# A decoder layer on one core: the layernorms' reciprocal root by Newton's method instead of ScalarE's Sqrt table

## The chip, the core and the metric

The kernel runs on one core of one Trainium2 chip. The core has five engines that run their own queues of instructions in order: TensorE (PE, matrix products and transposes; PEld is its loading of weights), VectorE (DVE), ScalarE (ACT), GpSimd (POOL) and SyncE (SP, which here issues most transfers). Engines wait for each other by semaphores. Operands lie in the on-chip memory SBUF (128 partitions); products land in PSUM, which has eight banks of 128 x 512 numbers.

The metric is device time in microseconds (us) of one execution. A profiled execution gives the rows quoted below. ScalarE computes a function such as exp, gelu or square root out of a table; where the next function lies in another table, the profile shows an ACT_TABLE_LOAD.

## The reference

A transformer decoder layer with normalisation ahead of each part, in f32, on x of shape (4, 1024, 256) and a context of (4, 64, 256):

```python
x = x + self_attention(layernorm(x))             # 16 heads of 16, 1024 x 1024 scores per head
x = x + cross_attention(layernorm(x), context)   # 16 heads of 16, 64 context tokens
x = x + ffn(layernorm(x))

def layernorm(x):  return (x - mean(x)) / sqrt(var(x) + 1e-5)
def self_attention(x):
    q, k, v = split(x @ W_qkv + b_qkv)
    return (softmax(q @ k.T) / 16 @ v) @ W_out + b_out       # per head
def ffn(x):
    h = gelu(x @ ternary(W_fc).T)
    h = layernorm(h) * ln_w + ln_b                          # over 1024
    return h @ ternary(W_proj).T
```

`ternary` turns a weight matrix into -1, 0 and 1 by a threshold from its mean absolute value. So each of the 4 batches has three layernorms of x (the first, second and third) and one of the hidden h.

## The kernel before

Tokens lie on partitions, 128 at a time: a batch b is NT = 8 tiles of 128 x 256. The work has three stages.

*The beginning* (to about 50 us) normalises batch 0, projects q and k of the first heads, and stores them to DRAM (`kept_q`, `kept_k`), from where `fetch(u)` brings them back in the layout of the scores, on SP's queue.

*The attention* (to about 1098 us) is a loop over 16 units u = (batch b, group g of four heads) of 16 steps each. A step makes scores for one pair of heads (`scores`, two products that each are followed by a product with `sel` and `mT`, which subtracts the row's maximum), exp on ACT (L888), the scores of the second pair and their exps, then `weigh`, which multiplies exps by the values into `ps_acc`. Between them `top()` makes scores of the next unit once more the other way round, only for the maxima that DVE reduces (L433). Scores, maxima and all side work share a ring of seven PSUM banks; PE waits when ACT or DVE has not yet emptied the bank that comes next.

The side work is written as generators in three lines. `due` holds `ln1(b)` (the first layernorm and the transposes of the next batch), `project` and `values`; `later` holds `context` and `value_bias` (once) and `post(b)` (output projection, second layernorm, cross-attention, statistics and root of the third layernorm); `aside` makes the ternary weights. `fill(kind, n)` is called twice a step and steps at most n of these generators to their next `yield`. A yield tagged "rows" or "cols" needs PE and a place of that kind; one tagged "free" has no product behind it, and each line takes at most one of these in a call. So a "free" yield that nothing stands behind is an empty place: it lets half a step go by.

The order on PE and SP is that of the program (`ordered`). The order on ACT, DVE and POOL is chosen by the framework's scheduler, from its own estimate of when operands are ready; it may move an instruction ahead of others written earlier.

*The last stage* (from about 1098 us) has the FFN in eight halves of four tiles: `widen(i)` normalises x with the kept root `rs3`, multiplies by `wfc`, applies gelu on ACT (L1001, tile `h`), takes the statistics (L1004, L1005), the root (L1007), the scale's product `nmr` (L1009), and normalises h, two tiles on DVE (L1012) and two on ACT (L1015). `narrow(i)` transposes h, splits it on ACT (`hT`, L1035) and DVE (`hl`, L1036) into a rounded part and its rest, and multiplies by `wproj`. A fixed list of places (`WIDE`, `NARROW`) puts them in each other's gaps, together with the rest of batch 3's `post`. There a step that is tagged "Gelu" or "Sqrt" is held back while a group of four cross-attention exps is open, so that their tables do not alternate (`apart`).

A layernorm is three helpers. `ln_stats` takes mean and variance on DVE (L233, L234: tile `mv`). `ln_rstd` (L236 to L240) makes the root on ACT (`sd`, with a table load at L239 where the table is another) and the reciprocal on DVE. `ln_normalised` (L242 to L260) makes `xn`: in the attention (`state["split"]`) by ACT as scale * x + bias (L250), with the bias `nmr` made on DVE (L246); elsewhere on DVE (L256).

POOL does little: copies of the cross-attention's weights (L463, `xwk` and `xwq`), `bv_wide` (L529), `lnb_wide` (L764), and the additions of the output biases to x (`add_row`, L280, with `bo`, `xbo` and `yrow`).

Of the kernel before, what the change touches and what calls it, by code (L numbers as in the profile page):

```python
# [8 lines left out]

F32 = mybir.dt.float32  # L10
F32R = mybir.dt.float32r
DRAM = bass.MemoryType.DRAM
AF = mybir.ActivationFunctionType
ALU = mybir.AluOpType
# [7 lines left out]
P = 128  # L22
NT = S // P
NG = 4
NU = B * NG
LN_EPS = 1e-5
# [4 lines left out]
def decoder_layer(ctx, tc, a, out):  # L31
# [48 lines left out]
    def xs(t, n=1):  # L80

        return x_of[t // NT][:, t % NT : t % NT + n, :]
# [95 lines left out]

    state = {"split": False, "banks": "ring"}

    def bank():
        return ps[state["banks"]]()
# [49 lines left out]
            nc.vector.bn_aggr(out=mv[:, i, :], in_=st)  # L234

    def ln_rstd(pool, rs, mv):  # L236
        n = mv.shape[1]
        sd = pool.tile([P, n], F32, tag="sd", name="sd", bufs=2)
        nc.scalar.activation(sd, mv[:, :, 1], AF.Sqrt, bias=eps_t[:, 0:1])  # L239
        nc.vector.reciprocal(out=rs, in_=sd)  # L240

    def ln_normalised(pool, mv, rs, i, t, n):  # L242
        xn = pool.tile([P, n, E], F32, tag="xn", name="xn", bufs=2)
        if state["split"]:
            nmr = pool.tile([P, n], F32, tag="nmr", name="nmr", bufs=2)
            nc.vector.scalar_tensor_tensor(  # L246
                nmr, mv[:, i : i + n, 0], -1.0, rs[:, i : i + n], ALU.mult, ALU.mult
            )
            for k in range(n):
                nc.scalar.activation(  # L250
                    xn[:, k, :], xs(t + k)[:, 0, :], AF.Identity, bias=nmr[:, k : k + 1],
                    scale=rs[:, i + k : i + k + 1],
                )
            return xn
        for k in range(n):
            nc.vector.tensor_scalar(  # L256
                xn[:, k, :], xs(t + k)[:, 0, :], mv[:, i + k, 0:1], rs[:, i + k : i + k + 1],
                ALU.subtract, ALU.mult,
            )
        return xn  # L260
# [63 lines left out]
    def ln1(b):  # L324
        mv = main.tile([P, NT, 2], F32, tag="mv1", name="mv1", bufs=2)
        rs = main.tile([P, NT], F32, tag="rs1", name="rs1", bufs=2)
        xnT_of[b] = xnT = main.tile([P, 2, S], F32, tag="xnT", name="xnT")
        n = NT if state["split"] else NT // 2
        for i0 in range(0, NT, n):
            for i in range(i0, i0 + n, 2):  # L330
                yield "free"
                ln_stats(main, mv, [(i + k, b * NT + i + k) for k in range(2)])
            yield "free"
            ln_rstd(main, rs[:, i0 : i0 + n], mv[:, i0 : i0 + n, :])
            for i in range(i0, i0 + n, 4):
                yield "free"
                xn = ln_normalised(post_pool, mv, rs, i, b * NT + i, 4)
                yield "rows"
                ln_transposed(xnT[:, :, i * P : (i + 4) * P], xn)

# [199 lines left out]
    def post(b):  # L540
# [20 lines left out]
        for i in range(0, NT, 2):  # L561
            yield "free"
            ln_stats(post_pool, mv, [(i + n, t0 + i + n) for n in range(2)])
        yield "free Sqrt"
        ln_rstd(post_pool, rs, mv)
        for half in range(2):
            h0 = half * 4
            xnT = post_pool.tile([P, 2, 512], F32, tag="xn2T", name="xn2T")
            yield "free"
            xn = ln_normalised(post_pool, mv, rs, h0, t0 + h0, 4)  # L570
            add_row(t0 + h0, xbo, 4)
            yield "rows"
            ln_transposed(xnT, xn)
            q2 = post_pool.tile([P, 2, 512], F32, tag="q2", name="q2")
            m = 256 if state["split"] else 512
            for i in range(0, 512, m):
                for c in range(2):
                    yield "cols+" if c or i else "cols"
                    head_proj(q2[:, c, :], late["xwq"], late["xbq"], c, xnT, slice(i, i + m))
            nm = post_pool.tile([P, 4, 2, 8], F32, tag="nm2", name="nm2")  # L580
            for t in range(4):
                yield "rows"
                pm = two_banks()
                for c in range(2):
                    for s in range(2):
                        r = slice(64 * s, 64 * s + 64)
                        matmul(
                            pm[s][:, c * 256 : (c + 1) * 256], lhsT=q2[r, c, t * P : (t + 1) * P],
                            rhs=kx[r, c, b, :, :].rearrange("p j k -> p (j k)"), start=True, stop=True,
                        )  # L590
                for s in range(2):
                    nc.vector.tensor_reduce(  # L592
                        nm[:, t, s, :], pm[s].rearrange("p (h k) -> p h k", k=SK), AX.X, ALU.max,
                        negate=True,
                    )
            yield "free"
            dst = nm_x[:, :, :, 0:8, :]
            nc.vector.tensor_copy(dst[:, :, :, :, 0].bitcast(F32R), nm)
            nc.vector.tensor_tensor(dst[:, :, :, :, 1], nm, dst[:, :, :, :, 0], ALU.subtract)
            yield "rows"  # L600
            views = turned([nm_x[:, t, :, :, :].rearrange("p s h l -> p (s h l)") for t in range(4)])
            mT = post_pool.tile([P, 512], F32R, tag="mTx", name="mTx")
            for r, v in enumerate(views):
                nc.scalar.copy(mT.rearrange("p (k r i) -> p r k i", r=len(views), k=4)[:, r, :, :], v)
            att = post_pool.tile([P, 4, NG, NG * D], F32, tag="attx", name="attx")
            before = None
            for g in range(NG):
                yield "rows+" if g else "rows"
                pe = two_banks()
                c, q = divmod(g, 2)  # L610
                sides = [(p, slice(64 * p, 64 * p + 64)) for p in range(2)]
                for p, r in sides:
                    matmul(
                        pe[p], lhsT=kx[r, c, b, 2 * q : 2 * q + 2, :].rearrange("p n k -> p (n k)"),
                        rhs=q2[r, c, :], start=True, stop=False,
                    )
                for p, r in sides:
                    matmul(
                        pe[p], lhsT=sel_x[r, 2 * g : 2 * g + 2, :].rearrange("p n k -> p (n k)"),
                        rhs=mT[r, :], start=False, stop=True,  # L620
                    )
                yield "free Exp"
                ex = post_pool.tile([P, 2, 512], F32, tag="xn2T", name="ex")
                for p in range(2):
                    nc.scalar.activation(ex[:, p, :], pe[p], AF.Exp, scale=0.25)  # L625
                if before is not None:
                    yield "rows"
                    normalised(*before)
                yield "cols"
                pa = bank()  # L630
                for j in range(NG):
                    matmul(
                        pa[32 * j : 32 * j + 32, :], lhsT=vx[:, b, 2 * g + j // 2, j % 2, :],
                        rhs=ex[:, j // 2, :], start=True, stop=True,
                    )
                oT = post_pool.tile([P, 512], F32, tag="oT", name="oT", bufs=2)
                nc.scalar.copy(oT, pa)
                before = att[:, :, g, :].rearrange("p t (j e) -> p t j e", j=NG), oT
            yield "rows"
            normalised(*before)  # L640
            yield from projected(
                lambda c, t: att[:, t, 2 * c : 2 * c + 2, :].rearrange("p g d -> p (g d)"),
                late["xwo"], t0 + h0, 4,
            )
        sl = slice(t0, t0 + NT)
        for i in range(0, NT, 2):
            yield "free"
            ln_stats(post_pool, mv3[:, sl, :], [(i + n, t0 + i + n) for n in range(2)])
        yield "free Sqrt"
        ln_rstd(post_pool, rs3[:, sl], mv3[:, sl, :])  # L650
        if b < B - 1:
            dma(out=x_kept[:, sl, :], in_=x_of[b])
# [174 lines left out]
        next(parts)  # L827
    run(first)
    run(parts)
    state["split"] = True  # L830
    run(fetch(0))

    sel_f = post_pool.tile([P, 2, P], F32, tag="xn", name="sel_f", bufs=2)
# [142 lines left out]
    def widen(i):  # L976
# [14 lines left out]
        for t in range(NH):  # L991
# [11 lines left out]
            for half in range(2):  # L1003
                nc.vector.bn_stats(out=st[:, half, :], in_=h[:, t, half * 512 : (half + 1) * 512])  # L1004
            nc.vector.bn_aggr(out=mv[:, t, :], in_=st)  # L1005
        yield "Sqrt"
        ln_rstd(ffn, rs, mv)  # L1007
        nmr = ffn.tile([P, NH], F32, tag="nmr", name="nmr", bufs=2)
        nc.vector.scalar_tensor_tensor(nmr, mv[:, :, 0], -1.0, rs, ALU.mult, ALU.mult)  # L1009
# [73 lines left out]
    while tag is not None or narrows:  # L1083
# [6 lines left out]
        if wides:  # L1090
            i = halves - len(wides)
            first = len(wides[0].places) <= len(WIDE) - 2
            late_x = i >= 2 * (B - 1) and tag is not None
            full = first and len(narrows) > halves + 1 - i
            apart = exps % NG and tag is not None and wides[0].tag in ("Gelu", "Sqrt")
            if not (late_x or full or apart):
                sources.append(wides[0])
        if narrows and len(narrows) > len(wides):
# [65 lines left out]
```

## Time and profile before

| | us |
|---|---|
| median of three runs | 1366.59 |
| lowest and highest | 1365.82, 1367.46 |
| the profiled execution | 1365.17 |
| its span | 1363.4 |
| table loads on ACT (43) | 1.283 each |
| root on ACT (`sd`, 21) | 0.30 each |
| reciprocal on DVE (`rs`, 21) | 0.18 to 0.19 each |
| `nmr` on DVE in the attention (12) | 0.154 each |
| addition of a bias on POOL, 128x512 | 1.30 each |

A row of the profile's groups names the source line, engine, operation, the tiles written and read, their shapes and the count; behind the first bar stand the busy time in us and the mean of one in ns, behind the second the idle time of the engine ahead of these instructions and what ended it. A row of the timeline gives start and duration in us, engine, line, operation, tiles and count; in brackets the idle time ahead of it and what ended that ("issue": nothing that the profile shows). The slices cut the span in 40; a digit is tenths of busy time, for PEclk tenths of the full clock of TensorE. The chain follows the work that ended last back to its start.

### The profile page before, as it was taken

To read this page: it belongs to the slowest core of one execution; us is meant where nothing else is said; L and a number is where in the kernel's file an instruction comes from. 1 tells how busy PE (TensorE), PEld (TensorE's weight loads), DVE (VectorE), ACT (ScalarE), POOL (GpSimd) and SP (SyncE) were. 2 spreads that over 40 slices of the span, in tenths; PEclk is the share of its full clock that TensorE was granted. 3 is DMA by queue.
4 is the path that set the end of the run, shared out by engine and by line. 5 is a ranking of instruction groups with operands and counts; after the bars stand their busy time and mean duration, and the time that the engine had idled before them with its cause. 6 is when DMAs were issued, how large, how long until landed. Compare 5 with 4: busy or idle time off the path is not lost.

```text
span 1363.4 us, 27651 instructions
## 1 busy us (share of the span) xinstructions
PE 1282.1 (94%) x11000; PEld 717.4 (53%) x11000; DVE 1004.7 (74%) x2110; ACT 898.5 (66%) x1654; POOL 80.0 (6%) x86
## 2 busy tenths in 40 slices
PE   3879999999999999999999999999999988999987
PEld 1434445545545454444545544545455466776777
DVE  4877777867878877877877777878889357565665
ACT  1377666756687667777676676676766746474765
POOL 4000000003010000011000000010000012000000
PEclk9889999999999999989999999999999989999989
DMA  5440312312130202131212112212210010100000
GB/s 169 126 143 30 111 42 68 94 48 63 41 85 1 63 7 57 33 93 31 64 35 60 38 27 75 82 53 73 55 40 1 2 62 1 44 19 31 1 31 32
DMA packets 46064, 72.72 MB, mean 53 GB/s; under 512 B 11280, under 2 KB 27920, under 8 KB 45936
## 3 DMA queue, kind: packets, MB, share of 16 engines
q1 hardware_dynamic: 44720, 68.47, 17.0%
q8 instruction: 87, 1.43, 0.4%
q10 hardware_dynamic: 1072, 2.10, 0.4%
q0 software_dynamic: 144, 0.39, 0.2%
q14 instruction: 41, 0.34, 0.1%
HBM read 46.81 MB, written 24.12 MB: 52 GB/s over the span
## 4 chain that ended last, share of the span: by engine, by line
PE 73%; DVE 16%; ACT 8%; issue 2%; DMA 1%; SPq 0%; DVEq 0%; ACTq 0%
PE ps_ring L57 42%; PE ps_acc L57 15%; PE ps_wide L57 8%; DVE mx L433 8%; PE ps_misc L57 3%; ACT exp L888 3%; PE ps_misc L60 2%; PE ps_ring L60 2%; DVE nm L592 2%; ACT xn L250 1%; DVE xn L256 1%; DVE bn L233 1%; DMA x<-in_x 1%; ACT ex L625 1%; ACT hl L359 1%
## 5 line engine op out<-in xcount | busy, mean ns | idle before, releaser
L433 DVE TENSOR_REDUCE mx<-ps_ring 128x1 f32<-128x512 f32 x1024 | 646.4, 682 | 157.6 <-PE ps_ring L57 156.7
L888 ACT ACTIVATE exp<-ps_ring 128x512 f32<-128x512 f32 x1024 | 549.2, 606 | 191.1 <-PE ps_ring L57 187.5
L57 PE MATMUL ps_ring<-q,k 64*128 64x512 f32 x1024 | 280.5, 474 | 8.0 <-ACT exp L888 5.9
L57 PE MATMUL ps_ring<-k,q 64*128 64x512 f32 x1024 | 260.2, 425 | 20.1 <-DMA q<-kept_q 7.9
L57 PE MATMUL ps_acc<-exp,v_sb 128*32 128x512 f32 x2048 | 275.3, 610 | 0.0
L57 PE MATMUL ps_ring<-mT,sel 64*128 64x512 f32 x1024 | 232.8, 400 | 0.2 <-ACT mT L451 0.2
L57 PEld LDWEIGHTS ps_ring<-q,k 64*128 64x128 f32 x1024 | 115.5, 185 | 198.4 <-ACT exp L888 69.0
L57 PEld LDWEIGHTS ps_ring<-k,q 64*128 64x128 f32 x1024 | 124.2, 186 | 100.2 <-ACT exp L888 41.3
L57 PEld LDWEIGHTS ps_ring<-mT,sel 64*128 64x128 f32 x1024 | 108.0, 186 | 6.3 <-ACT mT L451 0.7
L57 PEld LDWEIGHTS ps_acc<-exp,v_sb 128*32 128x32 f32 x2048 | 40.5, 108 | 67.4 <-issue 65.6
L1004 DVE BATCH_NORM_STATS2 bnh<-h 128x6 f32<-128x512 f32 x64 | 41.2, 679 | 34.1 <-ACT h L1001 34.0
L1001 ACT ACTIVATE h<-ps_wide 128x1024 f32<-128x1024 f32 x32 | 32.7, 1026 | 41.6 <-PE ps_wide L57 41.5
L1036 DVE SCALAR_TENSOR_TENSOR hl<-ps_misc,lnw,hT 128x512 fp32r<-128x512 f32 x64 | 46.4, 733 | 18.2 <-ACT hT L1035 18.2
L57 PE MATMUL ps_wide<-wproj,hl 128*128 128x256 f32 x256 | 46.2, 303 | 12.6 <-DVE hl L1036 12.5
L57 PE MATMUL ps_wide<-wfc,xl 128*128 128x512 f32 x128 | 56.5, 442 | 1.4 <-DVE xl L271 1.4
L57 PE MATMUL ps_wide<-wfc,xh 128*128 128x512 f32 x128 | 54.3, 424 | 0.0
L1035 ACT ACTIVATE hT<-ps_misc,lnw 128x512 fp32r<-128x512 f32 x64 | 42.6, 687 | 16.3 <-PE ps_misc L60 16.3
L233 DVE BATCH_NORM_STATS2 bn<-x 128x6 f32<-128x256 f32 x96 | 38.8, 416 | 8.1 <-DMA x<-in_x 6.4
L57 PEld LDWEIGHTS ps_wide<-wproj,hl 128*128 128x128 f32 x256 | 34.9, 191 | 16.2 <-DVE hl L1036 14.8
L280 POOL TENSOR_TENSOR x<-x,xbo 128x512 f32<-128x512 f32 x16 | 20.6, 1295 | 367.0 <-ACT xn L250 358.5
L57 PE MATMUL ps_wide<-wproj,hT 128*128 128x256 f32 x256 | 41.4, 284 | 0.0
L407 ACT COPY v_sb<-ps_ring 128x256 f32<-128x256 f32 x32 | 12.0, 375 | 41.0 <-PE ps_ring L57 30.6
(166 smaller groups left out, 1467.1 us busy)
## 6 DMA issues: line engine op xcount, KB each, us to landing
k<-kept_k SPq DMA_DIRECT2D x248, 64.0 KB
q<-kept_q SPq DMA_DIRECT2D x240, 64.0 KB
kept_q<-hl SPq DMA_DIRECT2D x15, 512.0 KB
kept_k<-hl SPq DMA_DIRECT2D x14, 512.0 KB
out<-x SPq DMA_DIRECT2D x16, 256.0 KB
x<-in_x SPq DMA_DIRECT2D x3, 1024.0 KB
x_kept<-x SPq DMA_DIRECT2D x3, 1024.0 KB
x<-x_kept SPq DMA_DIRECT2D x3, 1024.0 KB
```

What stands on the lines that cost most here:

```text
L57: ordered(nc.tensor.matmul(*args, **kwargs))
L60: ordered(nc.tensor.transpose(*args))
L233: nc.vector.bn_stats(out=st, in_=xs(t)[:, 0, :])
L250: nc.scalar.activation(xn[:, k, :], xs(t + k)[:, 0, :], AF.Identity, bias=nmr[:, k : k + 1], scale=rs[:, i + k : i + k + 1],)
L280: nc.gpsimd.tensor_tensor(xs(t, 2), xs(t, 2), row.rearrange("p (o d) -> p o d", o=1).to_broadcast([P, 2, E]), ALU.add,)
L433: nc.vector.tensor_reduce(mx[:, t, 2 * pair + n : 2 * pair + n + 1, kh], pm, AX.X, ALU.max)
L592: nc.vector.tensor_reduce(nm[:, t, s, :], pm[s].rearrange("p (h k) -> p h k", k=SK), AX.X, ALU.max, negate=True,)
L888: nc.scalar.activation(ex[:, n, :], pe[n], AF.Exp)
L1001: nc.scalar.activation(h[:, t, :], ph.rearrange("p a f -> p (a f)"), AF.Gelu)
L1004: nc.vector.bn_stats(out=st[:, half, :], in_=h[:, t, half * 512 : (half + 1) * 512])
L1035: nc.scalar.activation(hT, pt, AF.Copy, scale=w)
L1036: nc.vector.scalar_tensor_tensor(hl, pt, w, hT.bitcast(F32), ALU.mult, ALU.subtract)
```

## The change

Once the beginning is done (`state["table"]` becomes false), `ln_rstd` no longer uses ACT. It starts from an integer estimate of the reciprocal root, made on the bits of var + eps, and improves it by three rounds of Newton's method, r = r * (1.5 - 0.5 * v * r * r). In the attention these are 17 operations on POOL (3, three rounds of 4, and 2 that make `nmr` for all eight tiles at once); `ln1` and `post` then yield "free" four times before the first normalisation is put into the program. In the last stage they are 12 operations on DVE (3, and three rounds of 3). The tag "Sqrt" goes from the two places in `post` and from `widen`, and `apart` looks for "Gelu" alone. The third layernorm's root in `post`, which takes the same path, gets no empty places; its `nmr` is not used.

```diff
-    state = {"split": False, "banks": "ring"}
+    state = {"split": False, "banks": "ring", "table": True}
...
     def ln_rstd(pool, rs, mv):
         n = mv.shape[1]
-        sd = pool.tile([P, n], F32, tag="sd", name="sd", bufs=2)
-        nc.scalar.activation(sd, mv[:, :, 1], AF.Sqrt, bias=eps_t[:, 0:1])
-        nc.vector.reciprocal(out=rs, in_=sd)
-
-    def ln_normalised(pool, mv, rs, i, t, n):
+        if state["table"]:
+            sd = pool.tile([P, n], F32, tag="sd", name="sd", bufs=2)
+            nc.scalar.activation(sd, mv[:, :, 1], AF.Sqrt, bias=eps_t[:, 0:1])
+            nc.vector.reciprocal(out=rs, in_=sd)
+            return None
+        engine = nc.gpsimd if state["split"] else nc.vector
+        by = pool.tile([P, 3, n], F32, tag="sd", name="root", bufs=2)
+        var, half, t = (by[:, i, :] for i in range(3))
+        engine.tensor_scalar(var, mv[:, :, 1], LN_EPS, None, ALU.add)
+        engine.tensor_scalar(half, var, -0.5, None, ALU.mult)
+        engine.tensor_scalar(
+            rs.bitcast(I32), var.bitcast(I32), -0.5, float(0x5F3759DF), ALU.mult, ALU.add
+        )
+        for _ in range(3):
+            engine.tensor_tensor(t, rs, half, ALU.mult)
+            engine.tensor_tensor(t, t, rs, ALU.mult)
+            if state["split"]:
+                engine.tensor_scalar(t, t, 1.5, None, ALU.add)
+                engine.tensor_tensor(rs, rs, t, ALU.mult)
+            else:
+                engine.scalar_tensor_tensor(rs, t, 1.5, rs, ALU.add, ALU.mult)
+        if not state["split"]:
+            return None
+        nmr = pool.tile([P, n], F32, tag="nmr", name="nmr", bufs=2)
+        engine.tensor_tensor(nmr, mv[:, :, 0], rs, ALU.mult)
+        engine.tensor_scalar(nmr, nmr, -1.0, None, ALU.mult)
+        return nmr
+
+    def ln_normalised(pool, mv, rs, i, t, n, nmr=None):
         xn = pool.tile([P, n, E], F32, tag="xn", name="xn", bufs=2)
-        if state["split"]:
-            nmr = pool.tile([P, n], F32, tag="nmr", name="nmr", bufs=2)
-            nc.vector.scalar_tensor_tensor(
-                nmr, mv[:, i : i + n, 0], -1.0, rs[:, i : i + n], ALU.mult, ALU.mult
-            )
+        if nmr is not None:
...
-            ln_rstd(main, rs[:, i0 : i0 + n], mv[:, i0 : i0 + n, :])
+            nmr = ln_rstd(main, rs[:, i0 : i0 + n], mv[:, i0 : i0 + n, :])
+            for _ in range(4 if nmr is not None else 0):
+                yield "free"
...
-        yield "free Sqrt"
-        ln_rstd(post_pool, rs, mv)
+        yield "free"
+        nmr = ln_rstd(post_pool, rs, mv)
+        for _ in range(4 if nmr is not None else 0):
+            yield "free"
...
-        yield "free Sqrt"
+        yield "free"
         ln_rstd(post_pool, rs3[:, sl], mv3[:, sl, :])
...
-    state["split"] = True
+    state.update(split=True, table=False)
...
-        yield "Sqrt"
+        yield ""
         ln_rstd(ffn, rs, mv)
...
-            apart = exps % NG and tag is not None and wides[0].tag in ("Gelu", "Sqrt")
+            apart = exps % NG and tag is not None and wides[0].tag == "Gelu"
```

More of the change, by code (lines that the diff above doesn't have):

```diff
@@ L11 @@
 F32R = mybir.dt.float32r
+I32 = mybir.dt.int32
 DRAM = bass.MemoryType.DRAM
@@ L249, in ln_normalised @@
+        if not state["split"]:
[5 more added lines that the diff above has]
+    def ln_normalised(pool, mv, rs, i, t, n, nmr=None):
+        xn = pool.tile([P, n, E], F32, tag="xn", name="xn", bufs=2)
+        if nmr is not None:
             for k in range(n):
                 nc.scalar.activation(
-                    xn[:, k, :], xs(t + k)[:, 0, :], AF.Identity, bias=nmr[:, k : k + 1],
+                    xn[:, k, :], xs(t + k)[:, 0, :], AF.Identity, bias=nmr[:, i + k : i + k + 1],
@@ L333, in ln1 @@
             yield "free"
-            ln_rstd(main, rs[:, i0 : i0 + n], mv[:, i0 : i0 + n, :])
+            nmr = ln_rstd(main, rs[:, i0 : i0 + n], mv[:, i0 : i0 + n, :])
+            for _ in range(4 if nmr is not None else 0):
+                yield "free"
             for i in range(i0, i0 + n, 4):
                 yield "free"
-                xn = ln_normalised(post_pool, mv, rs, i, b * NT + i, 4)
+                xn = ln_normalised(post_pool, mv, rs, i, b * NT + i, 4, nmr)
                 yield "rows"
@@ L569, in post @@
             yield "free"
-            xn = ln_normalised(post_pool, mv, rs, h0, t0 + h0, 4)
+            xn = ln_normalised(post_pool, mv, rs, h0, t0 + h0, 4, nmr)
             add_row(t0 + h0, xbo, 4)
```

## The prediction

> **What bounds the kernel now.** I read the page's share of busy time first, then the slices, the chain, the groups of ScalarE (ACT), and last the timeline around each root.
>
> ```profile
> span 1363.4 us, 27651 instructions
> PE 1282.1 (94%) x11000; PEld 717.4 (53%) x11000; DVE 1004.7 (74%) x2110; ACT 898.5 (66%) x1654; POOL 80.0 (6%) x86
> PEclk9889999999999999989999999999999989999989
> PE 73%; DVE 16%; ACT 8%; issue 2%; DMA 1%; SPq 0%; DVEq 0%; ACTq 0%
> ...
> L239 ACT ACT_TABLE_LOAD x20 | 25.7, 1283 | 1.1 <-PEq L1153 0.7
> L1001 ACT ACT_TABLE_LOAD x12 | 15.4, 1283 | 4.1 <-PE ps_wide L57 3.9
> L888 ACT ACT_TABLE_LOAD x9 | 11.5, 1283 | 0.2
> ```
>
> TensorE (PE) is the bound: 94% busy, 73% of the chain. ACT has 34% idle, so the 52.6 us of these three groups of table loads are mostly no part of the time; only PE's gaps and half-clock stretches can be won. PE is idle 18.8 us between 100 and 1098 us (attention) and 28.4 us from there to the end. Measured as step lengths (one step is 2.88 us plus its fill work), the attention steps around the roots are 15.6 us too long in all, leaving the first root out. The stretch at 578 us shows the kind:
>
> ```profile
> 574.38 1.28 ACT L239 ACT_TABLE_LOAD   x1
> 575.68 0.30 ACT L239 ACTIVATE sd<-mv,eps_t 128x8 f32<-128x8 f32 x1
> 576.53 1.28 ACT L888 ACT_TABLE_LOAD   x1
> 578.47 0.50 PE L57 MATMUL ps_ring<-q,k 64*128 64x512 f32 x1 [0.95 <-ACT exp L888]
> ```
>
> A load for the root, the root, a load back: 1.28 + 0.30 + 1.28 = 2.87 us in which ACT makes no exp, and here PE runs dry for 0.95 us. The clock granted at 579.45 us falls to 0.5 for 3.41 us, which costs some 1.7 us more.
>
> **What the change removes.** In the order of its instructions, table loads fall from 43 to 7 and 19 of the 21 roots leave ACT: 36 x 1.283 + 19 x 0.30 = 52 us of ACT. [...]
>
> **What it adds on GpSimd (POOL).** 17 operations for each of nine layernorms, each waiting for the one before (but the one on the integer view). No row of before shows such an operation. From below: the 128x1 MEMSET takes 0.103 us, 17 x 0.103 = 1.75 us. From above: the 128x512 addition takes 1.295 us, 17 x 1.295 = 22 us. The nearest rows are small copies, back to back every 186 ns, and the start of a POOL operation 0.13 us after its releaser:
>
> ```profile
> 79.79 1.49 POOL L463 COPY xwk<-xwk_in 128x64 f32<-128x64 f32 x8 [58.35 <-DMA xwk_in<-in_xwk]
> 1047.31 0.15 DVE L748 TENSOR_SCALAR thr<-thr 128x1 f32<-128x1 f32 x1
> 1047.50 0.15 DVE L749 TENSOR_SCALAR thr<-thr 128x1 f32<-128x1 f32 x1
> ```
>
> 1.49/8 = 0.186, plus 0.12 to 0.13 for the wait: an estimate of 0.305 us for a dependent operation, 5.2 us for a root. The two last lines are the same kind of chain on VectorE (DVE): 0.19 us apart. So my plausible ends are 0.19 (3.2 us) and 0.5 (8.5 us). [...]
>
> **Part by part, in the attention.** The four empty places do not do what they count: the scheduler that fills ACT's queue puts the first normalisation (xn) soon after the place of the old root. Counted in exps on ACT, for batch 0's second layernorm the root stood at exp 304 and the xn's at 310 to 316; now they stand at 306 to 312.
>
> First root (82 us, ln1(1)):
>
> ```profile
> 81.88 1.28 ACT L239 ACT_TABLE_LOAD   x1
> 83.26 1.05 PE L57 MATMUL ps_ring<-ctx_in,xwk 128*32 128x256 f32 x16
> 91.43 0.20 DVE L240 RECIPROCAL rs<-sd 128x8 f32<-128x8 f32 x1 [3.96 <-ACT sd L239]
> 93.88 0.76 PE L57 MATMUL ps_ring<-k,q 64*128 64x512 f32 x1 [7.24 <-issue]
> ```
>
> ACT made eight xn's and a second root (ln1(2)), DVE waited 3.96 us for that root with the kx products behind it, and PE stood 7.24 us. All that goes. But on POOL's queue both roots now stand ahead of the xwk copies (and of xwq's copies, bv_wide and the bo additions, which nobody wants soon). Root 1 runs from 82.1 to 87.3, root 2, whose statistics are ready about 87.4, to 92.6, the copies take 1.5: 94.1. PE waits for them at the product of ctx_in and xwk, where it arrives at 83.26; from there it has 3.4 us of work (83.26 to 86.65) to where it now resumes at 93.88. 94.1 + 3.4 = 97.5 against 93.88: +3.4 to +3.6, I take +3.4. By 0.2 us an operation it is +1.6, by 0.4 +6.8.
>
> Second layernorm of batches 0, 1, 2 (372, 631, 896 us):
>
> ```profile
> 372.74 1.28 ACT L239 ACT_TABLE_LOAD   x1
> 374.35 1.28 ACT L888 ACT_TABLE_LOAD   x1
> 375.65 2.06 ACT L888 ACTIVATE exp<-ps_ring 128x512 f32<-128x512 f32 x4
> ```
>
> The statistics end at 372.48, POOL at 372.5 + 5.2 = 377.7. ACT has two exps to do first and reaches the xn at about 374.05, so it waits 3.65 us where it lost 2.87 before: +0.75. Behind it in ACT's queue stand the exps that empty PSUM for PE. Then five xn's of 0.57 us stand among the next six exps, where there were none; half of them I count as uncovered: +1.45. So +2.2 for batch 0 and for batch 2, which has the same order. In batch 1 four exps come first (wait 2.6 us, -0.3) and then four xn's in a row, +2.0: +1.7. Sum +6.1; each 0.1 us on an operation is 1.7 us at each of the three.
>
> Third layernorm (574, 842 us): its root is wanted only in the last stage, so the load pair goes with nothing in its place. At 574 the gap of 0.95, the half clock's 1.7 and some 0.85 of the long step: -3.5. At 842 the step is 1.53 too long: -1.4. The one at the end of batch 2 likewise lies beside other work. ln1(3) at 589: the half clock at 593.10 (1.7) may go, and the xn's then wait for POOL behind four exps: -1.5, give or take 2.
>
> Queues otherwise: PE's order shifts its fill work by one to two and a half steps, on SP one kept_q store goes behind four groups of q and k fetches, wanted steps later: nothing, and at worst one fetch late, about 1 us. On POOL the last root stands behind lnb_wide (1054.66), hidden by 40 us of attention.
>
> Attention: 3.4 + 6.1 - 4.9 - 1.5 = +3.1. With 0.2 us an operation it is about -3.8, with 0.4 about +13.
>
> **Last stage (from 1098 us).** PE's order stays. ACT loses about 20 loads and 11 roots, 29 us; DVE gets ten roots of 12 operations at 0.19, less the reciprocals: +21 us, put between its own work. What a place wins or loses is PE's gap there:
>
> ```profile
> 1142.58 1.19 PE L57 MATMUL ps_wide<-wproj,hl 128*128 128x256 f32 x4 [3.65 <-DVE hl L1036]
> 1200.91 1.26 DVE L1009 SCALAR_TENSOR_TENSOR nmr<-mvh,rsh 128x4 f32<-128x4 f32 x1
> 1322.83 0.74 PE L57 MATMUL ps_wide<-wproj,hl 128*128 128x256 f32 x4 [2.89 <-DVE hl L1036]
> ```
>
> The 3.65 us (hl behind a root and six xn's on DVE) goes: -3.9 with what is around it. Half 4 (1271): the gap of 1.07 behind a load goes, less 0.6: -0.5. Half 6: hl comes ahead of the normalisation, 2.89 to 0.75, of which 1.4 returns: -0.7. Against that, in half 7 the load was hidden: statistics to normalised scale took 1.43 us (1341.48 to 1342.91) and now take 13 x 0.19 plus the DVE work between, 4.4 us; the transposes go from 1346.1 to 1348.3: +2.0. Half 5 with batch 3's third layernorm likewise +1.5. Halves 0, 2, 3: +0.3, +0.6, +0.5. Sum -0.2, give or take 4. The nmr above took 1.26 us in place of 0.16 while POOL added yrow: a root of 12 operations meets such an addition once at most, in some of the ten places, which is the upper side of the 4.
>
> **Sum.** +3.1 - 0.2 = +2.9 on the profiled execution's 1365.17 us (1363.4 and 1.8 around it): 1368.1. That execution is 1.4 us under the median of the runs, so against the median 1366.59 I say **1369.5**. About 0.2% (2.7 us) is what a measurement can tell from no change here.
>
> **Rivals.** *The chain on POOL is short* (0.2 us an operation, near VectorE's 0.19): then it ends within the 2.87 us of the pair that it replaces and the long steps are won. Attention -3.8, last stage -4 by its better end: -8, 1358.6. It decides from 0.26 us an operation downwards, where my sum is zero. For it: the 0.103 us MEMSET. Against: 0.186 for a copy without any wait.
> *The chain is long* (0.4 or more, 6.8 us): ACT stalls at each second layernorm and the copies of xwk come at 97: +13, 1379.6; at 0.5 some +20. For it: 262 to 296 ns for a 64x32 MEMSET.
> *VectorE becomes the bound of the last stage*: 21 us more on an engine busy 170 of 265 us, and 1.1 us for each meeting with POOL: +7, with the attention at +3: 1376.5. Against: PE's gaps behind hl become fewer in its order.
> *Nothing shows*: PE at 94% hides loads and waits alike, 1366.6.
>
> **How the numbers follow.** Forecast 0.36 (own range 1366 to 1374: slower 0.24, same 0.10, faster 0.02); short chain 0.29 (faster 0.28, same 0.01); long chain 0.18; VectorE 0.10; nothing 0.07 (same 0.05, a hundredth or so to either side). Faster 0.31, same 0.16, slower 0.53. The range leaves out the case in which all gaps go (-12) and the chain beyond 0.45 us: 1356 to 1384.
>
> **What would show it.** Seven table loads. POOL's 17 operations about 0.3 us apart; ACT waiting 3 to 4 us for POOL's nmr ahead of xn near 374 and 898; PE waiting for xwk's copies until about 94; no half clock at 579. In the last stage operations 0.19 us apart on DVE with single ones of 1.2, no gap of 3.65 at 1139, the last transposes 2 us later. Operations under 0.26 us apart, or exps that stay ahead of the waiting xn's, would make it wrong.

## The result and the profile after

The changed kernel took 1374.15 us (median of four runs, 1372.53 to 1374.84) against 1366.66 for the kernel before: a ratio of 1.0057, 95% interval 1.0043 to 1.0072, so 7.5 us slower. Forecast were 2.9 us slower. The two profiled executions are 1374.54 and 1365.17 us, 9.4 apart; all differences of places below are between these two.

The page of the changed kernel, and below the dots its groups of table loads on ScalarE:

```profile
span 1372.8 us, 27834 instructions
PE 1286.1 (94%) x11000; PEld 718.2 (52%) x11000; DVE 1017.4 (74%) x2199; ACT 850.5 (62%) x1599; POOL 113.0 (8%) x239
PE 74%; DVE 17%; ACT 4%; DMA 2%; issue 1%; POOL 1%; SPq 0%; DVEq 0%; ACTq 0%; POOLq 0%
...
L1030 ACT ACT_TABLE_LOAD x3 | 3.8, 1283 | 5.0 <-PE ps_wide L58 5.0
L654 ACT ACT_TABLE_LOAD x2 | 2.6, 1283 | 0.0
L245 ACT ACT_TABLE_LOAD x1 | 1.3, 1283 | 0.7 <-PEq L1182 0.7
L917 ACT ACT_TABLE_LOAD x1 | 1.3, 1283 | 0.0
```

Seven loads are left, ACT is busy 48 us less, its share of the chain falls from 8% to 4%, and the time grows. POOL now stands in the chain, and DMA has 2% of it in place of 1%. The groups of POOL give the price of one operation of the root, and the table of waits (in all, times, longest) what ACT pays for the whole:

```profile
L260 POOL TENSOR_SCALAR root<-root 128x8 f32<-128x8 f32 x27 | 6.4, 236 | 2.4
L257 POOL TENSOR_TENSOR root<-rs,root 128x8 f32<-128x8 f32 x27 | 5.5, 203 | 2.2
...
ACT xn L275 <- POOL nmr L268: 17.9, 5, 4.3
```

0.20 to 0.24 us each, and with the wait 0.28 to 0.32 from start to start: a root of 17 took 4.95 us (373.28 to 378.23). ACT waited for it five times, 17.9 us in all. The timeline at batch 0's second layernorm (start, duration, engine, operation; in brackets the wait and what ended it):

```profile
373.01 0.18 DVE L235 BATCH_NORM_AGGREGATE mv<-bn 128x2 f32<-128x6 f32 x1
373.64 1.09 ACT L917 ACTIVATE exp<-ps_ring 128x512 f32<-128x512 f32 x2 [0.21 <-PE ps_ring L58]
377.99 0.24 POOL L268 TENSOR_SCALAR nmr<-nmr 128x8 f32<-128x8 f32 x1
378.26 0.60 ACT L275 ACTIVATE xn<-x,nmr,rs 128x256 f32<-128x256 f32 x1 [3.54 <-POOL nmr L268]
379.40 0.50 PE L58 MATMUL ps_ring<-k,q 64*128 64x512 f32 x2 [2.09 <-ACT exp L917]
382.23 1.25 PE L58 MATMUL ps_ring<-k,q 64*128 64x512 f32 x2 [1.61 <-DVE hl L387]
```

ACT does two exps and stands 3.54 us in front of an xn. The exps queued behind it keep PSUM full, and PE waits 2.09 us for one of them; then it waits 1.61 us for `hl` on VectorE, whose input ACT makes only between the xn's. Then two products that took 0.50 us take 1.25: the granted clock is 0.5 from 382.11 for 6.83 us. The kernel before lost 0.31 and 1.26 us at this place and kept its clock:

```profile
382.02 0.49 PE L57 MATMUL ps_ring<-k,q 64*128 64x512 f32 x1 [0.31 <-ACT exp L888]
386.77 0.53 PE L57 MATMUL ps_ring<-q,k 64*128 64x512 f32 x2 [1.26 <-ACT exp L888]
```

The largest loss is elsewhere, at 590 us, and no root is in its first gap. First the changed kernel, then the one before:

```profile
581.77 0.38 SPq L64 DMA_DIRECT2D x_kept<-x  x1
586.66 0.39 SPq L64 DMA_DIRECT2D x<-in_x  x1
592.51 0.75 DVE L234 BATCH_NORM_STATS2 bn<-x 128x6 f32<-128x256 f32 x2 [2.78 <-DMA x<-in_x]
596.33 0.79 PE L58 MATMUL ps_ring<-q,k 64*128 64x512 f32 x1 [3.52 <-DVE mx L460]
```

```profile
573.21 0.38 SPq L63 DMA_DIRECT2D x_kept<-x  x1
578.00 0.39 SPq L63 DMA_DIRECT2D x<-in_x  x1
584.14 0.74 DVE L233 BATCH_NORM_STATS2 bn<-x 128x6 f32<-128x256 f32 x2
```

Batch 0's x is stored, batch 3's x is loaded into the same buffer, and ln1(3)'s statistics read it: 10.7 and 10.9 us from the store's issue to the first statistic, the same in both. Before, VectorE came to the statistic just then. Now it waits 2.78 us, does eight statistics with the maxima queued behind them, PE stands 3.52 us, and the clock is 0.5 for 6.83 us from 593.74. Behind that ACT waits 3.11 us for this layernorm's root, and PE 1.81 us.

Measured at the same steps of the program in both traces (steps are counted through from 0 to 255, each from the first product of its `weigh`). As the side work stands at other steps in the two kernels, the lag swings by 1 to 2 us from step to step, so a single line is good to about 1 us:

| place | forecast | measured |
|---|---|---|
| first root and all up to 329 us | +3.4 | +0.7 |
| second layernorm, batches 0, 1, 2 | +2.2, +1.7, +2.2 | +2.9, +2.7, +2.7 |
| third layernorm, 574 and 842 us | -3.5, -1.4 | -2.5, +0.2 |
| ln1(3), 590 us | -1.5 | +4.3 |
| last stage | -0.2 | -1.8 |
| sum (with +0.1 in the rest) | +2.9 | +9.4 |

### The profile page after: what moved, and what is told of

It reads as the page before. It is cut to its first block, busy times and chain, and to the rows that moved or that the text cites. A ratio compares the mean times of both kernels' runs of the same rounds, so it can differ in the third digit from the quotient of the medians.

```text
span 1372.8 us, 27834 instructions
## 1 busy us (share of the span) xinstructions
PE 1286.1 (94%) x11000; PEld 718.2 (52%) x11000; DVE 1017.4 (74%) x2199; ACT 850.5 (62%) x1599; POOL 113.0 (8%) x239
## 4 chain that ended last, share of the span: by engine, by line
PE 74%; DVE 17%; ACT 4%; DMA 2%; issue 1%; POOL 1%; SPq 0%; DVEq 0%; ACTq 0%; POOLq 0%
PE ps_ring L58 45%; PE ps_acc L58 17%; DVE mx L460 7%; PE ps_wide L58 6%; PE ps_ring L61 2%; PE ps_misc L58 2%; PE ps_misc L61 2%; DVE nm L621 2%; DVE bnh L1033 1%; DVE bn L234 1%; DMA x<-in_x 1%; ACT exp L917 1%; DVE hl L1065 1%; DVE xn L281 1%; DVE xl L296 1%
## 5 line engine op out<-in xcount | busy, mean ns | idle before, releaser
L58 PE MATMUL ps_ring<-k,q 64*128 64x512 f32 x1024 | 266.1, 429 | 24.2 <-ACT exp L917 10.1
L58 PEld LDWEIGHTS ps_ring<-k,q 64*128 64x128 f32 x1024 | 127.2, 188 | 107.4 <-ACT exp L917 49.6
L61 PE MATMUL ps_misc<-ident,h 128*128 128x128 f32 x256 | 40.0, 284 | 5.2 <-DVE h L1041 2.3
L387 DVE SCALAR_TENSOR_TENSOR hl<-ps_ring,bq_c,hl 128x256 f32<-128x256 f32 (+1 forms) x30 | 15.0, 500 | 36.2 <-ACT hl L386 36.2
```

Of the source, the lines that this page charges most:

```text
L58: ordered(nc.tensor.matmul(*args, **kwargs))
L61: ordered(nc.tensor.transpose(*args))
L387: nc.vector.scalar_tensor_tensor(hl[:, 1, part], pq, bias, hl[:, 0, part], ALU.add, ALU.subtract)
```

## The experiments

The theory was A: all of the loss is in the attention, by three mechanisms. W: ACT waits for POOL at the second layernorms. P, later L: the load of batch 3's x. C, which came up on the way: VectorE and GpSimd hinder each other. The rivals are named in each expectation.

**One part of the change at a time.** The attention's part alone:

```diff
-    state.update(split=False, banks="misc")
+    state.update(split=False, banks="misc", table=True)
...
-        yield ""
+        yield "Sqrt"
         ln_rstd(ffn, rs, mv)
...
-            apart = exps % NG and tag is not None and wides[0].tag == "Gelu"
+            apart = exps % NG and tag is not None and wides[0].tag in ("Gelu", "Sqrt")
```

> Newton's method on GpSimd in the attention only; the last stage has ScalarE's Sqrt table as before. Theory A (all of the loss arises in the attention, and the last stage gives a little back: by the steps of the two traces +11.2 us up to 1100 us and -1.8 after it): 1366.7 + 9 to 11 = 1376 to 1378 us, slower than the changed kernel. Rival B (the last stage, with 21 us more on VectorE, has a share in the loss): under 1374.

1382.68 us (1377.56 to 1385.80), ratio 1.0127 (1.0107 to 1.0146). And the last stage's part alone, which is the kernel before with the root on VectorE, its tags, and this after the attention:

```diff
-    state.update(split=False, banks="misc")
+    state.update(split=False, banks="misc", table=False)
```

> Newton's method on VectorE in the last stage only; the attention as before. Theory A: 1366.7 - 1.8 = 1365 us, 1363 to 1366. Rival B: 1367 to 1370. In the profile the 3.65 us gap of TensorE at 1139 us goes under both; the last half's transposes come 2 us later.

1363.81 us, ratio 0.9989 (0.9980 to 0.9998). The last stage gains 1.6 us; A holds, B (a share of the loss in the last stage) falls. The attention's part alone was expected at 1376 to 1378, and only its lowest run, the profiled one, lies there. Four of its five runs lie at 1382 to 1386.

**Without the places in post.**

```diff
         nmr = ln_rstd(post_pool, rs, mv)
-        for _ in range(4 if nmr is not None else 0):
-            yield "free"
```

> The changed kernel without the four empty places in post; those in ln1 stay. Theory P: the places hold post(0) back by 2 to 2.5 steps, so batch 0's x is stored later, the load of batch 3's x into the same buffer is issued later, the statistics of ln1(3) on VectorE wait 2.8 us for it with the maxima queued behind them, and TensorE stands 3.5 us at 593 us and then runs at half clock for 6.83 us. Then without the places that wait and gap go: 3.5 + 3.4/2 to 3.4 less, 1374.2 - 4 to -7 = 1367 to 1370 us. Rival Q (the load is late because the whole timeline or the queues are, not by the places): within 1 us of 1374.

1380.03 us (1374.77 to 1385.42), ratio 1.0102 (1.0073 to 1.0131), in two groups, 1375 and 1385. P falls as it was put. Without the places the store does go back by 4.15 us against the steps (1.67 us ahead of step 126, as in the kernel before; 2.48 us behind it in the changed one). But VectorE comes to the statistics earlier by as much, 6.3 us behind step 126 in place of 10.4: from the store to its coming are 8.0 us in both kernels, and it still waits, here 4.2 us. What is left as the difference to the kernel before is the time of the two steps from 126 to 128: 9.26 us there, with the third layernorm's table loads and a half clock in them, 6.3 us here. So the removed stall seems to have hidden the load. That is theory L, below.

The last stage's part alone, whose attention is that of the kernel before, shows that the half clock in the stall was part of the cover. Its trace has the table loads and PE's gap of 0.96 us at 577 us, but no half clock behind it, and the wait is there:

```profile
578.33 0.50 PE L58 MATMUL ps_ring<-q,k 64*128 64x512 f32 x1 [0.96 <-ACT exp L902]
584.61 0.75 DVE L234 BATCH_NORM_STATS2 bn<-x 128x6 f32<-128x256 f32 x2 [2.09 <-DMA x<-in_x]
```

Against the trace of before it is 1.3 us ahead by step 128 and loses 3.1 by step 131, with a half clock of 6.83 us from 586.44. So an execution without the half clock at 579 lost more than it won, with no change in the attention at all.

**ScalarE in program order.**

```diff
+    def put(*args, **kwargs):
+        ordered(nc.scalar.activation(*args, **kwargs))
...
-                nc.scalar.activation(
+                put(
                     xn[:, k, :], xs(t + k)[:, 0, :], AF.Identity, bias=nmr[:, i + k : i + k + 1],
...
-            nc.scalar.activation(ex[:, n, :], pe[n], AF.Exp)
+            put(ex[:, n, :], pe[n], AF.Exp)
```

> The changed kernel with the exps and the normalisations (xn) kept in program order on ScalarE, so that the four empty places hold on its queue and each xn stands at least eight exps behind the root. Theory W (at each second layernorm ScalarE waits 3.5 us for GpSimd's nmr with exps queued behind it, and TensorE's gaps there bring 6.83 us of half clock; +2.7 us each): these waits go, -8 us, 1366 us, give or take 2. Rival V (it isn't the wait but the xn's themselves, 8 x 0.57 us among the exps, that cost): no more than -3, 1371 or above.

Ratio 1.0019 (1.0003 to 1.0035), in two groups again: three runs at 1361.4 to 1363.7, nine at 1367.8 to 1371.6. The profile is of a lower run. The wait for nmr is gone from its waits; in batch 0 the first four xn's stand 18 exps later, the other four 98 exps behind these. Against the kernel before, batch 0's second layernorm now gains 3.0 us and batch 2's 2.3, where the changed kernel lost 2.9 and 2.7. So W holds, and is worth 5 to 6 us at each of these two places; but the xn's also stand apart now, so this run does not separate the wait from V (the xn's among the exps cost, not the wait). The next one does. All runs taken together, the median moved by 4 us and not by 8: the upper group had to be understood first.

**A shorter chain.**

```diff
-        for _ in range(3):
+        for _ in range(2 if state["split"] else 3):
```

> The changed kernel with two rounds of Newton's method in place of three on GpSimd (the last stage keeps three), so that the root is less exact and the chain is 4 operations of 0.29 us, 1.16 us, shorter; the order on ScalarE is the same but for two xn's. Theory W (ScalarE's wait for nmr sets the loss at each second layernorm): its longest waits fall from 3.5 to 4.3 us to 2.4 to 3.1, and 0.7 to 1.2 us is gained at each of four places; the xwk copies end 2.3 us earlier: 1374 - 4 to -6 = 1368 to 1370 us in the lower group. Rival V (the xn's among the exps cost, not the wait): 1372 to 1375, the shorter wait gives nothing.

Twelve runs: 1365.8 to 1368.8 and 1373.6 to 1378.0, ratio 1.0042 (1.0023 to 1.0061) over both. The table of waits of a lower run:

```profile
ACT xn L275 <- POOL nmr L268: 11.9, 5, 3.1
```

Five waits as before, 6.0 us less in all, and the lower group is some 6 us under the changed kernel's. W again, V falls. Against the changed kernel 1.3, 2.5 and 1.6 us are gained at the three second layernorms, and 1.8 us at the first root, where the copies come earlier. 1.16 us on the chain buys more than 1.16 us at a place where the half clock, at 643 and 909 us, lasts 3.41 us in place of 6.83.

**The two groups.** The changed kernel once more, and then with GpSimd's additions in order:

> The changed kernel itself once more, beside the next three on the same chip. Two of the kernels run so far fell into two groups of times: without the places 1375 and 1385 us, with ScalarE in order 1361 to 1364 and 1368 to 1372. In the profile of an upper one VectorE's cast of the negative maxima (nm_s) takes 7.44 us at 319 us, until GpSimd's row of twelve bo additions (14.9 us) ends; in lower ones it gets in between two additions after 1.3 us. Theory C (a race for the way to memory between the two engines): the changed kernel has both outcomes too, 1373 to 1375 and 1382 to 1385. Rival D (the two groups come from something else that those kernels changed): all runs at 1372 to 1375.

Six runs: 1372.57 to 1375.23 four times, 1382.47 and 1384.11. The profile is of the last. In its timeline:

```profile
311.10 14.90 POOL L305 TENSOR_TENSOR x<-x,bo 128x512 f32<-128x512 f32 x12 [76.52 <-DVE bo L562]
318.57 7.47 DVE L472 CAST nm_s<-nm 128x16 fp32r<-128x16 f32 x1
326.07 0.18 DVE L473 TENSOR_TENSOR nm_s<-nm,nm_s 128x16 f32<-128x16 f32 x1
326.30 0.69 PE L61 MATMUL ps_ring<-ident,nm_s 64*128 64x64 f32 x8 [5.63 <-DVE nm_s L473]
```

A cast of 16 columns that otherwise takes 0.17 us takes 7.47 and ends at 326.04; the twelve additions end at 326.00. PE waits 5.63 us and comes back at half clock for 6.83 (two products of 0.50 us take 0.78), and from step 60 to 64 this execution loses 7.7 us on the first profile of the same kernel. There the cast took 1.30 and the subtraction behind it 1.22. In the kernel before the additions began at 303.9, and the cast met only the last of them. First the changed kernel's first profile, then the kernel before:

```profile
310.23 14.95 POOL L305 TENSOR_TENSOR x<-x,bo 128x512 f32<-128x512 f32 x12 [76.44 <-DVE bo L562]
317.69 1.30 DVE L472 CAST nm_s<-nm 128x16 fp32r<-128x16 f32 x1
```

```profile
303.89 14.97 POOL L280 TENSOR_TENSOR x<-x,bo 128x512 f32<-128x512 f32 x12 [28.21 <-DVE bo L535]
318.03 0.87 DVE L445 CAST nm_s<-nm 128x16 fp32r<-128x16 f32 x1
```

The additions wait for `bo`, which now comes 6.3 us later, and so they fall onto the cast.

```diff
+            add = on_pool.tensor_tensor if state["split"] else nc.gpsimd.tensor_tensor
-            nc.gpsimd.tensor_tensor(
+            add(
                 xs(t, 2), xs(t, 2),
```

Here `on_pool` puts `ordered` around an operation; the roots of post go through it too.

> The changed kernel with the bo additions and the roots of post kept in program order on GpSimd, so that only four additions (5 us) stand together at 310 us and end before the cast at 317.7. Theory C: no run above 1376, median 1371 to 1374 (the 2.3 us that the cast and the subtraction behind it were held in the lower case also go). Rival D: the same two groups as the changed kernel.

1373.12 us (1371.98 to 1374.65), ratio 1.0057 (1.0044 to 1.0070).

```profile
308.31 5.04 POOL L239 TENSOR_TENSOR x<-x,bo 128x512 f32<-128x512 f32 x4 [76.88 <-DVE bo L569]
315.76 0.17 DVE L479 CAST nm_s<-nm 128x16 fp32r<-128x16 f32 x1
```

The additions are over when the cast comes; no run is in an upper group. Five runs alone say little, where the changed kernel had two upper ones in ten. But the two mended kernels below, with the additions in order too, have none in nine, where the kernel with ScalarE alone in order had nine of twelve. C holds as to the times; that the race is one for the way to memory was the author's guess, and no run shows it. Two more profiles are of upper runs, and both show the same: the kernel without the places (7.44 us) and the one with late statistics (7.43). In the lower runs the meeting costs PE nothing that shows: without it this kernel gains nothing on the changed one from step 56 to 64.

**The load of batch 3's x.**

```diff
     def ln1(b):
...
+        for _ in range(8 if b == 3 else 0):
+            yield "free"
```

> The changed kernel with eight empty places ahead of ln1(3)'s statistics, so that VectorE reaches them some four steps (12 us) later. Theory L (the store of batch 0's x and the load of batch 3's x into the same buffer take 11 to 12 us one behind the other; before the change the third layernorm's table loads hid them, now VectorE waits for the load with the maxima queued behind): the wait at 592 us and TensorE's gap of 3.5 us behind it go, with the half clock there: 3.5 + 1.7 to 3.4 less than the changed kernel on this chip, and no DMA wait in front of the statistics. Rival M (the load only covers another lateness, such as the root of ln1(3) on GpSimd): less than 2 us gained, a gap of the same size a little later.

1379.17 us (1376.17 to 1386.56), ratio 1.0104 (1.0081 to 1.0127): a miss that tells nothing of L. The scheduler put the first statistic back to where it had been, 560 maxima into its queue, and the wait stayed at 3.06 us. So, with the late places, the statistics of ln1(3) and the maxima were kept in program order:

```diff
-            nc.vector.bn_stats(out=st, in_=xs(t)[:, 0, :])
+            stats = nc.vector.bn_stats(out=st, in_=xs(t)[:, 0, :])
+            if pool is main and t // NT == 3:
+                ordered(stats)
...
-                        nc.vector.tensor_reduce(
+                        ordered(nc.vector.tensor_reduce(
```

> As the kernel with late statistics (eight empty places ahead of ln1(3)'s statistics), but these statistics and the maxima are kept in program order on VectorE: in the earlier try the scheduler put the first of them back to where it had been, six maxima earlier than the program has it, and the wait for the load stayed (3.06 us). Theory L: now VectorE comes to the first statistic 4 to 5 us later, the wait falls under 0.5 us and TensorE's gap behind the maxima (2.5 to 4 us) goes. The gap behind ScalarE's xn wait 14 us later stays, so over both 1 to 4 us are gained against the changed kernel's 1372.5 to 1375 in its lower group. Rival M: a gap of the same size stays ahead of the next step.

1380.17 us (1379.89 to 1381.56), ratio 1.0112 (1.0097 to 1.0127). At the place L holds: no wait for the load, no gap, and from step 128 to step 131 the kernel gains 8.4 us on the changed one. Three steps later 8.5 us are given back:

```profile
611.03 4.04 ACT L277 ACTIVATE xn<-x,nmr,rs 128x256 f32<-128x256 f32 x8 [5.06 <-POOL nmr L270]
615.23 0.17 DVE L775 MEMSET ones<- 128x128 f32 x1 [7.24 <-ACT xn L277]
615.99 0.58 PE L61 MATMUL ps_ring<-ident,nm_s 64*128 64x64 f32 x6 [7.68 <-DVE mx L464]
```

The root comes later and ACT stands in front of the xn's for 5.06 us; a small MEMSET on VectorE that takes over a buffer of this layernorm waits for all eight of them, and the maxima wait behind it. The gap was expected to stay and grew. A second loss of some 4.4 us stands at 950 us, where VectorE waits 6.30 us for a weight's load; the kernel with late statistics alone does not have it.

**All mended.** ScalarE in order, additions in order, the late places, and GpSimd's roots and `xwk` copies in program order, with the `xwq` weights twelve steps later so that their copies do not stand ahead of the first root:

```diff
+                    if name == "xwk":
+                        ordered(copied)
...
+        for _ in range(12):
+            yield
         late["xwq"] = const.tile([P, 2, E], F32, name="xwq")
```

> All together: exps and normalisations in program order on ScalarE; the xwk copies, roots and bo additions in program order on GpSimd, the copies ahead of the first root and those of xwq after it (its load twelve steps later); eight empty places ahead of ln1(3)'s statistics. From the changed kernel's 1374: second layernorms -11 to -15 (from the kernel with ScalarE in order, whose lower group is at 1362.5), statistics of ln1(3) -5, xwk copies 0 to -5, no upper group. Theories W, L and C together: 1352 to 1358 us, faster than the kernel before. Rival: the copies or the later places block something else, 1360 or above.

1351.83 us (1350.51 to 1352.47), ratio 0.9899 (0.9885 to 0.9912): faster than both kernels. Its page and its first root:

```profile
span 1348.7 us, 27848 instructions
PE 1278.0 (95%) x11000; PEld 716.2 (53%) x11000; DVE 1015.0 (75%) x2199; ACT 848.1 (63%) x1599; POOL 112.9 (8%) x239
...
78.21 1.48 POOL L502 COPY xwk<-xwk_in 128x64 f32<-128x64 f32 x8 [56.03 <-DMA xwk_in<-in_xwk]
89.80 0.76 PE L58 MATMUL ps_ring<-k,q 64*128 64x512 f32 x1 [3.07 <-DVE kx L543]
```

The copies are made when their data come, and PE's gap is 3.07 us, against 7.24 in the kernel before and 9.15 in the changed one:

```profile
87.80 4.04 ACT L275 ACTIVATE xn<-x,nmr,rs 128x256 f32<-128x256 f32 x8 [4.31 <-POOL nmr L268]
92.95 1.49 POOL L490 COPY xwk<-xwk_in 128x64 f32<-128x64 f32 x8
93.24 2.09 PE L58 MATMUL ps_ring<-ctx_in,xwk 128*32 128x256 f32 x16 [9.15 <-POOL xwk L490]
```

By step 16 the mended kernel is 6.2 us ahead of the kernel before, and the one with ScalarE alone in order 0.25 behind; 1.0 us of that stands already at step 0, so the copies' place is worth 5.5 us. Its statistics still wait 5.0 us for the load, PE 4.46: of the 5 us that were expected here only a part came. With the maxima in order as well:

> The kernel with all mended, with ln1(3)'s statistics and the maxima in program order on VectorE as well. Its wait of 5.0 us for the load and TensorE's gap of 4.46 us go, and the half clock of 3.41 us behind them. Theory L: 1351.8 - 4 to 6 = 1346 to 1348 us. Rival M: 1350 to 1353.

1355.88 us (1354.01 to 1357.18), ratio 0.9930 (0.9918 to 0.9943), a miss. At the place 6.1 us are won against the kernel with all mended (steps 128 to 131), as L has it, and 2.0 of them are given back by step 136. And 6.6 us are lost between 220 and 300 us, where the roundings of k and q on ACT now wait 3.40 us twice for a store to free their buffer. The order that mends one place moves another.

**Is it the order alone?** The kernel before, with its table, with exps, roots and normalisations in program order:

> The kernel before, with its Sqrt table, with exps, roots and normalisations kept in program order on ScalarE. Theory R (the gain of the mended kernel comes from the root without the table, once the places hold): the 36 loads stay, 1362 to 1368 us. Rival S (it comes from the order of ScalarE alone): 1355 or less.

1376.46 us (1370.47 to 1377.26), ratio 1.0073 (1.0056 to 1.0089). S (the gain is ScalarE's order alone) falls. R's own number was missed too, by 8 us: in this order the statistics of ln1(3) wait 2.69 us for the load and PE runs at half clock for 13.65 us from 587.88. But at the first root this order gains with the table as well: PE's gap there is 3.07 us as in the mended kernel, and from step 0 to 16 it wins 3.4 us on the kernel before, where the mended kernel wins 6.7:

```profile
88.28 0.47 PE L57 MATMUL ps_ring<-k,q 64*128 64x512 f32 x1 [3.07 <-DVE kx L505]
```

So ScalarE's order alone does not gain with the table; what GpSimd's order and the late places would gain with it was not run, and how much of the mended kernel's 13 us is the root's is open.

## Why the prediction was right and wrong

- *The sign held, and the wide range* (1356 to 1384); 1374.15 lies just above the forecast's own range of 1366 to 1374. The size was too small: +2.9 forecast, +7.5 by the medians. Between the two traces three terms are too low by 10.6 us together (second and third layernorms, ln1(3)), and two too high by 4.3 (first root, last stage). That these took off part of the error was luck.
- *The price of an operation on POOL*: 0.305 us estimated, 0.29 measured; a root 5.2 forecast, 4.95 measured. The estimate from copies (0.186 us) and a start 0.12 to 0.13 us behind the releaser was good.
- *The second layernorms*: the mechanism was right, batch 0's wait of 3.65 us was 3.54, and the term was too small by 0.5 to 1.0 us at each place. Batch 1's wait was forecast at 2.6 us and was 3.42. The half clock was counted where it would go, at 574 and 593, and not beside PE's new gaps, where the trace now has it: 6.83 us each from 382.11, 644.93 and 911.17.
- *The step that failed, ln1(3)*: forecast -1.5, measured +4.3, the largest error of the sum. The gain at 574 came nearly as said (-2.5 for -3.5), and what stood behind it was not asked: a store and a load, 11 us one behind the other, that the removed stall had covered. The half clock that "may go" came back longer, 6.83 us for 3.41. Not all of it need be the change's: the trace with the attention as before loses 3.1 us there as well.
- *A step costed at nothing*: "PE's order shifts its fill work by one to two and a half steps ... nothing, and at worst one fetch late". The shift moved the `bo` additions from 303.9 to 310.2, onto the cast. In most runs that costs PE nothing that shows, so it is no part of the measured 7.5 us, and in some 7.7 us.
- *At 842 us* 1.4 us were forecast as gain and none came. Why was not tested.
- *The first root*: PE held for the copies, as forecast, until 93.24 (the copies were over at 94.44, forecast 94.1), and at the next step the lag was +3.0, of which 0.6 stood there already at step 0, for +3.4. But by 131 us it had been made good (-0.15), which the forecast did not have, and up to 329 us the sum is +0.7, with the 0.6 and the additions' meeting in it. Why it was made good was not tested.
- *The last stage*: -0.2 forecast, -1.8 in the traces and -1.6 by its own run. The gap of 3.65 us went, but three gaps of 1.15, 1.12 and 0.88 us, in which PE waits for xn's, stand at the same place (1152 to 1157); the gaps of 2.24 us (1296) and 2.89 (1320) of before are none and 1.54. Roots' operations took 1.2 to 1.3 us beside `yrow` and `xbo` additions six times, as the trace of before had shown for nmr. That a root meets such an addition "once at most" was wrong: one met two (1159.13 and 1160.79).
- *The rivals*: the short chain (0.2 us) and the long one (0.4) are excluded by 0.29 us an operation; VectorE as bound of the last stage is excluded by the run of that part alone.

## What to carry to other kernels

A removed stall can have been the cover of something: before booking its gain, look for the transfer or the wait that ended beneath it, and measure from its issue how long it takes. Where a scheduler orders a queue, empty places in the program are no places on the engine; keep in program order what must stay apart, look at what else moves, and weigh a moved piece by whom it will meet and not only by who waits for it.

## What the runs showed that was not expected

A small operation on VectorE ended only with a row of GpSimd's: the 0.17 us cast took 7.47 us under twelve additions of 1.25 us each (its end 326.04, theirs 326.00), or 1.30 us, in different executions of the same kernel, which fell into two groups 7 to 10 us apart.

The subtraction behind it took 1.22 us beside additions and 0.18 without. 7.47 us are the time of six of these additions, 1.30 that of one. For what the two engines contend no run shows.

In the attention behind 100 us, PE's gaps of 3.52 and 4.09 us in the changed kernel (to 596.33 and 645.23) overlap with a clock of 0.5 that lasted 6.83 us each (from 593.74 and 644.93); beside the gap of 4.03 us in the kernel with two rounds it lasted 3.41. Smaller gaps had it or not: 0.95 us at 577 us in the kernel before was followed by 3.41 us of it, from 579.45; 1.26 us there (to 386.77), 1.81 us in the changed kernel (to 604.52), 0.96 us at 577 us in the last stage's part alone and 2.27 us at 611 us in the changed kernel once more were not. In these numbers neither the half clock nor its length follows from the gap alone.
